# Who turns the attention squares: PE, or VectorE with a way through DRAM, in a two-layer graph kernel

## The chip, the cores and the metric

The kernel runs on one core of a Trainium2 chip. Its time is device microseconds of one execution. The engines are PE (TensorE; PEld is its weight loads), DVE (VectorE), ACT (ScalarE), POOL (GpSimd) and SP (SyncE, which here only issues DMAs).

## The reference

Layer 0 is a graph attention layer over 4096 nodes with 256 features and a dense 0/1 adjacency. Layer 1, where the change lies, does two steps of a top-p attention and of a graph walk:

```python
def _top_p_attention(X, W1, W2, W3):
    q = X @ W1.T @ W2.T
    k = X @ W3.T
    probs = softmax(q @ k.T / TAU, axis=-1)
    # keep, in every row, the largest probabilities up to a sum of TOP_P = 0.9
    ...
    A = probs * mask
    return A / maximum(A.sum(-1, keepdims=True), 1e-12)

R = S + eye(N);  R = R / R.sum(-1, keepdims=True)
Z = 0;  Xf = X;  Xa = X
for n in range(2):
    A = _top_p_attention(Xa, W1, W2, W3)
    Xf = R @ Xf
    Xa = A @ Xa
    Z = Z + Xf @ U1[n].T + Xa @ U2[n].T
h = X + Z
return (h - mean(h)) / sqrt(var(h) + LN_EPS) * ln_g + ln_b
```

Each layer is entered through a normalization and a relu, and added to its input.

## The kernel before

The 4096 rows are 32 blocks of 128 (NB = 32). The kernel's stages follow each other: layer 0, the first hop (`R @ X`, `graph_products`), step 0's attention over the 32 blocks, the second hop with the projections of step 1 put between its products, step 1's attention. Nearly all of it is under a manual schedule: every engine executes its instructions in the order in which the program writes them, and waits at the head of its queue for what it needs.

**One block of attention.** For block b, `exponentials` (ACT) makes the row block e of 128 x 4096 f32 from the logits (PE, `logits`). ACT counts against a first threshold (`first_probe`, four passes of 2048 columns), POOL works out the next threshold in some fifteen tiny instructions (`first_step`, its result is the tile c), DVE filters with it (`third_probe`, line L1015 in the profile, 128x4096), finds the cut (`candidates`: 18 MAX8 over the filtered row, then a chain of small operations, L1033 to L1052, with L1049 and L1050 in it), and zeroes what is under the cut (`masked`, L1058, 128x4096, in place in e). Then e is the left operand of `A @ X`, and PE needs it with the 4096 columns on the partitions: `turn` transposes four squares of 128x128 (L1124) into a PSUM tile and ACT copies them to SBUF (eT, L1126); `gather` multiplies them with four blocks of X and accumulates (L1132; each f32 product shows as two matmuls). There are eight such groups g of four squares.

**The order around it.** For each b the program writes `chosen_kept(b)` and then `attend(b)`:

```python
for b in range(NB - 1):
    chosen_kept(b)
    if b + AHEAD < NB:
        blocks[b + AHEAD] = began(n, b + AHEAD, G)
    attend(blocks[b], cur, blocks.get(b + AHEAD),
           beside.get(b, {}), [first] if b == 0 else ())
```

`attend(b)` has PE turn and gather block b, with the logits, exponentials and probes of block b + 3 (AHEAD) put between the groups; group g + 2 is turned before group g is gathered. `chosen_kept(b)` writes, in this order, candidates of b, `polished` of b - 3 (step 1: two POOL rows L1333 and L1334 and the output's DMA), third_probe of b + 1, `finish` of b - 2 (DVE: L1311 in step 0 with a store of z; L1314 and two statistics in step 1), `finish_scale` of b - 2 (POOL L1321 to L1325), `first_step` of b + 2 (POOL), `gathered` of b - 1 (step 1: three POOL rows L1150 to L1152), and masked of b (DVE). Blocks 0 to 2 of each step have their cut found earlier, in the hop before (`picks`). `began` loads the next query through SP (`swapped`), `loads` (SP) brings xf, and in step 1 v, z and x1.

**The states' products.** At the start of step 1, `projections` multiplies each block of the attention's states with both U2 matrices (`carried`, PE L797). Half of the result, v, is copied by ACT (L799) and stored by an ACT DMA; the other half replaces the states (DVE copy, L801). All this lies between the products of the second hop, whose own operands DVE and ACT prepare (L467, L468, five buffers).

Of the kernel before, what the change touches and what calls it, by code (L numbers as in the profile page):

```python
# [26 lines left out]
P = 128  # L27
# [29 lines left out]
def gat_then_top_p_diffusion(  # L57
# [100 lines left out]

    uv_d = dram.tile([H, P, NB, 2, W3 + 1], BF16, name="uv_d")
    s_d = dram.tile([H, N], F32, name="s_d")  # L160
    adj_d = dram.tile([NB // G0, P, NB, G0 * P], F32R, name="adj_d")
    with tc.tile_pool(name="l0", bufs=1) as l0, tc.tile_pool(name="l0s", bufs=2) as l0s, tc.tile_pool(name="l0o", bufs=1) as l0o:
        passing = ctx.enter_context(ExitStack())
# [613 lines left out]
    def projections(cur, n, G):  # L777
# [10 lines left out]
        lengths = small.tile([P, NB, 2], F32, name="lengths", bufs=1)  # L788
        u2 = S.u2.pop() if n > 0 else None

        def carried(xs, g, i):
            if n == 0:
                return
            b = 4 * g + i
            pt = ps3.tile([P, 4, P], F32, name="tp").rearrange("p a b -> p (a b)")
            for k in range(KC):
                nc.tensor.matmul(pt, xs[:, k, i, :], u2[:, k].rearrange("p n m -> p (n m)"), start=(k == 0), stop=(k == KC - 1))  # L797
            v = rows.tile([P, D], F32, name="part", bufs=3)
            nc.scalar.copy(v, pt[:, :D])  # L799
            nc.scalar.dma_start(block(v_d, b), v)  # L800
            nc.vector.tensor_copy(cur[:, b, :], pt[:, D:])  # L801

        for g in range(NB // 4):
            xs = l1e.tile([P, 3, 4, P], F32, name="xs", tag="e1")
# [250 lines left out]
    def masked(r):  # L1055

        kept, r.scale = col("kept"), col("scale")
        nc.vector.scalar_tensor_tensor(r.e, r.e, r.t, r.e, ALU.is_ge, ALU.mult, accum_out=kept)  # L1058
        nc.vector.reciprocal(r.scale, kept)
# [24 lines left out]
    def untied(r, z, work):  # L1084
# [18 lines left out]
        nc.vector.scalar_tensor_tensor(r.e, ties, r.t, r.e, ALU.mult, ALU.add, accum_out=kept)  # L1103
        nc.vector.reciprocal(r.scale, kept)

    def block(t, b):
        return t[ds(b, 1)].rearrange("o p d -> (o p) d")

    def loads(r):
        r.xf, r.part = rows.tile([P, KC, P], F32, name="xf"), rows.tile([P, D], F32, name="part", bufs=3)  # L1110
        nc.sync.dma_start(r.xf, xft_d[r.n][ds(r.b, 1)].rearrange("o p s i -> (o p) s i"))
        if r.n > 0:
            r.v = rows.tile([P, D], F32, name="xa")
            nc.sync.dma_start(r.v, block(v_d, r.b))
            nc.sync.dma_start(r.part, block(z_d, r.b))
            r.x1 = rows.tile([P, D], F32, name="x1", bufs=3)
            nc.sync.dma_start(r.x1, block(x1_d, r.b))
        r.acc = ps1.tile([P, 2, D], F32, name="acc")
        r.far = r.acc[:, 1, :]
# [9 lines left out]
    def gather(r, eT, g, cur):  # L1129
        for i in range(4):  # L1130
            j = 4 * g + i
            nc.tensor.matmul(r.acc[:, 0, :], eT[:, i, :], cur[:, j, :], start=(j == 0), stop=(j == NB - 1))  # L1132

    def scaled(r):
        if r.n + 1 < STEPS:
# [11 lines left out]

    def gathered(r):
        if r.n + 1 == STEPS:
            nc.gpsimd.tensor_tensor(r.part, r.part, r.v, ALU.add)  # L1150
            nc.gpsimd.tensor_tensor(r.x1, r.x1, ln_b_r, ALU.add)
            nc.gpsimd.tensor_tensor(r.part, r.part, r.xf.rearrange("p k i -> p (k i)"), ALU.add)  # L1152

    def attend(r, cur, ahead, between={}, eT=()):

        if ahead:
            ahead.pm = {}
        def start(c):
            if ahead:
                ahead.pm[c] = logits(ahead.q, ahead.kT, c)  # L1160
                exponentials(ahead, c)
        eT = list(eT) or [turn(r, 0)]
        start(0)
        loads(r)
        r.ri = rinv[:, r.b:r.b + 1]
        last = r.n + 1 == STEPS and r.b + 1 == NB
        if last:
            r.far = bank()[:, :D]
        eT.append(turn(r, 1))
        start(1)  # L1170
        for g in range(NB // 4):
            if g + 2 < NB // 4:
                eT.append(turn(r, g + 2))
            gather(r, eT[g], g, cur)
            if last and g == 4:
                contributed(r)
                weighed(r)
                gathered(r)
            if g < 2:
                start(2 + g)  # L1180
            elif g == 2 and ahead:
                summed(ahead)
            elif g in PROBED and ahead:
                first_probe(ahead, PROBED.index(g))
            if g in between:
                between[g]()
        if not last:
            contributed(r)
            weighed(r)
        scaled(r)  # L1190
# [193 lines left out]
    for n in range(STEPS):  # L1384
        cur = X
        G = SimpleNamespace()
        found = [table(f"found{i}") for i in range(3)]
        blocks = {}
        with tc.manual_schedule(engines=every):
            pieces = first_hop if n == 0 else hops(second)  # L1390
            filling, picking = fills(n, G, found, blocks), picks(n, found, blocks)
            done = 0 if n else NB - G0 - LOOK
            for i, _ in enumerate(pieces, 2 * done):
                if n > 0 and i % 6 == 1 and i // 6 < NB // 4:
                    g = i // 6
                    nc.sync.dma_start(cur[:, ts(g, 4), :], xa_d[ts(g, 4)].rearrange("b p d -> p b d"))
                if (n == 0 or i > 10) and i // 2 % NB != NB - 2:
                    next(filling, None)
                    if i // 2 % NB < NB - 3 or i % (2 * NB) == 2 * NB - 1:
                        next(picking, None)  # L1400
                if i == 2 * len(order) - 6:
                    first = turn(blocks[0], 0)
            weights(n)
            for _ in filling:
                next(picking, None)
            for _ in picking:
                pass

            def chosen_kept(b):

                r = blocks[b]
                if not hasattr(r, "kept"):
                    candidates(r, found)
                if b > 2:
                    polished(blocks.pop(b - 3))
                if b + 1 < NB and not hasattr(blocks[b + 1], "thirded"):
                    third_probe(blocks[b + 1])
                if b > 1:
                    finish(blocks[b - 2])
                    finish_scale(blocks[b - 2])  # L1420
                if b + 2 < NB and not hasattr(blocks[b + 2], "stepped"):
                    first_step(blocks[b + 2])
                if 0 < b < NB - 1:
                    gathered(blocks[b - 1])
                if not hasattr(r, "kept"):
                    masked(r)
                if 1 < b < NB - 1:
                    normal(blocks[b - 2])

            R = SimpleNamespace(n=n, kT=G.kT, qT=G.qT, nm=G.nm, table=found[0])  # L1430

            def last_chosen():
                chosen_kept(NB - 1)
                R.failed, R.undone = questioned(G, found)

            def looked():
                counted(R)
                chosen(R)

            def beginning():  # L1440
                normal(blocks[NB - 3])
                gathered(blocks[NB - 2])
                finish(blocks[NB - 2])
                finish_scale(blocks[NB - 2])

            def asked():
                R.count = number(R, R.undone)

            beside = {NB - 2: {5: last_chosen}, 0: dict(zip((0, 1, 3, 5, 6), S.turned))}
# [6 lines that stand above are left out]
            r = blocks[NB - 1]  # L1456

            def earlier():
                polished(blocks[NB - 3])
                finish_rows(blocks[NB - 2])  # L1460

            beside = {0: beginning, 1: looked, 3: earlier, 4: asked}
            if n + 1 < STEPS:
                second = hop_of(n + 1)
                beside.update({2: lambda: (both_weights(), begin(second, 5)), 5: lambda: split(second, 2), 6: lambda: (split(second, 5), own(second, 5))})
            attend(r, cur, None, beside)
            for m in range(second.begun if n + 1 < STEPS else 0):
                for s in range(KC):
                    graph_products(second, m, s, (0,))
            finish(r)  # L1470
            finish_scale(r)
            finish_rows(r)
        repaired(R, cur)
# [32 lines left out]
```

## Time and profile before

| | |
|---|---|
| median of 3 runs | 2820.71 us (2817.5 to 2821.74) |
| the profiled execution | 2820.09 us, span of its instructions 2818.1 us |
| granted TensorE clock, mean | 0.996 |
| L1132, gather | x4096, 948.0 us busy on PE |
| L1124, transposes | x2048, 306.4 us busy on PE |
| L1126, copies of the transposed squares | x512, 297.0 us busy on ACT |
| L1015 and L1058, third_probe and masked | x58 each, 261.4 and 259.0 us busy on DVE |
| step 0's attention, from block 0's end to block 31's | 1095.99 to 1766.81 us |
| step 1's attention, the same | 2136.86 to 2804.30 us |

The busy time of a group is the time in which at least one of its instructions ran; PE's matmuls overlap, so 948.0 us for 4096 is 0.23 us each though one lasts 0.38. Idle time is put down to what released the engine last. The time of an execution lies some 2 us above the span.

### The profile page before, as it was taken

The page shows a single profiled execution, that of the slowest core. Times are in us where ns is not written, and L with a number is a line of the kernel's source. Part 1 is how long each engine was busy: PE and PEld are TensorE (multiplying, and loading weights), DVE is VectorE, ACT ScalarE, POOL GpSimd, SP SyncE. Part 2 cuts the span into 40 slices and gives each one's busy share as a digit, 9 for nine tenths or more (in the row PEclk, how much of TensorE's full clock was granted, in tenths as well). Part 3 has the DMA queues.
Part 4 walks back from the last instruction along what each step waited for, and adds up shares of the span by engine and source line. Part 5 has one row for each costly group of instructions (what it writes and reads, how often), then busy time and mean ns, then how long its engine had stood idle before and what let it go on. Part 6 is the DMA issues. An engine that isn't in the chain of part 4 may idle for free. (4 is left out here: it accounts for less than half of the span.)

```text
span 2818.1 us, 51577 instructions
## 1 busy us (share of the span) xinstructions
PE 2772.0 (98%) x18791; PEld 2443.1 (87%) x18791; DVE 2164.6 (77%) x5067; ACT 1925.4 (68%) x3066; POOL 907.2 (32%) x1895
## 2 busy tenths in 40 slices
PE   6999999999999999999999999999999999999998
PEld 5899999999988888888888888667878888888887
DVE  8877878778654385999989997333574999999997
ACT  8867886879633636888888884232627878887882
POOL 7311121111011231223332231000304666666664
PEclk9999999999999999999999999999999999999999
DMA  9969597695376782000000002667991111111110
GB/s 204 255 247 197 210 233 196 228 203 217 143 229 213 242 305 94 21 21 21 27 20 21 21 24 69 217 196 239 332 348 50 32 34 40 31 32 32 37 34 26
DMA packets 174114, 376.44 MB, mean 134 GB/s; under 512 B 18198, under 2 KB 123542, under 8 KB 169750
## 3 DMA queue, kind: packets, MB, share of 16 engines
q1 hardware_dynamic: 142496, 271.12, 29.9%
q0 software_dynamic: 26112, 97.53, 13.8%
q10 hardware_dynamic: 5238, 4.35, 0.5%
q8 instruction: 153, 2.51, 0.4%
q14 instruction: 115, 0.94, 0.1%
HBM read 305.48 MB, written 113.57 MB: 149 GB/s over the span
## 5 line engine op out<-in xcount | busy, mean ns | idle before, releaser
L1132 PE MATMUL acc<-X,eT 128*128 128x256 f32 x4096 | 948.0, 379 | 0.0
L1132 PEld LDWEIGHTS acc<-X,eT 128*128 128x128 f32 x4096 | 748.1, 190 | 85.7
L400 PE MATMUL acc<-ut,m 128*128 128x195 bf16 (+1 forms) x8192 | 698.1, 246 | 1.2 <-DVE m L379 0.9
L400 PEld LDWEIGHTS <-m 128*128 128x128 fp8e4 x8192 | 696.8, 97 | 2.4 <-DVE m L379 1.5
L372 ACT ACTIVATE g<-sr,d_big 128x1024 uint8<-128x1024 f32 x448 | 473.0, 1135 | 9.9 <-DVE m L378 9.9
L947 ACT ACTIVATE e<-mm,nm 128x1024 f32<-128x1024 f32 x256 | 286.4, 1119 | 178.3 <-PE mm L763 167.4
L1126 ACT COPY eT<-tp 128x512 f32<-128x512 f32 x512 | 297.0, 581 | 80.1 <-PE tp L1124 79.8
L1033 DVE MAX8 cand<-big 128x8 f32<-128x228 f32 (+1 forms) x1152 | 348.3, 380 | 0.0
L646 PE MATMUL mm<-ar,hl 128*128 128x512 f32 x848 | 336.4, 407 | 3.8 <-DMA ar<-adj_d 1.7
L1015 DVE SCALAR_TENSOR_TENSOR big<-e,c 128x4096 f32<-128x4096 f32 x58 | 261.4, 4506 | 87.0 <-POOL c L1000 56.9
L646 PE MATMUL acc<-ar,hl 128*128 128x512 f32 x848 | 324.1, 393 | 1.3 <-DVE ar L490 1.3
L1124 PE MATMUL tp<-ident,e 128*128 128x128 f32 x2048 | 306.4, 273 | 5.3 <-ACT eT L1126 3.1
L1124 PEld LDWEIGHTS tp<-ident,e 128*128 128x128 f32 x2048 | 254.2, 141 | 65.7 <-ACT eT L1126 4.5
L378 DVE TENSOR_TENSOR m<-g,ax 128x512 uint32<-128x512 uint32 x256 | 188.7, 737 | 97.4 <-PE acc L400 76.9
L1058 DVE SCALAR_TENSOR_TENSOR e<-e,found 128x4096 f32<-128x4096 f32 x58 | 259.0, 4466 | 0.0
L954 ACT ACTIVATE void<-e,c 128x2048 int8<-128x2048 f32 x128 | 257.0, 2008 | 0.9
L954 ACT ACTIVATE void<-e,c1x 128x2048 int8<-128x2048 f32 x128 | 256.9, 2007 | 0.9
L971 POOL TENSOR_TENSOR sums<-sums 128x2 f32<-128x2 f32 x64 | 12.7, 199 | 623.7 <-ACT void L954 622.2
L379 DVE TENSOR_TENSOR m<-m,ax 128x512 uint32<-128x512 uint32 x256 | 183.2, 715 | 25.7 <-PE acc L400 0.5
L646 PEld LDWEIGHTS mm<-ar,hl 128*128 128x128 f32 x848 | 159.6, 188 | 43.7 <-issue 9.5
L763 PE MATMUL mm<-kT,qT 128*128 128x512 f32 x512 | 192.4, 457 | 1.5 <-ACT e L947 1.5
L646 PEld LDWEIGHTS acc<-ar,hl 128*128 128x128 f32 x848 | 159.3, 188 | 37.7 <-issue 4.1
(311 smaller groups left out, 3525.6 us busy)
## 6 DMA issues: line engine op xcount, KB each, us to landing
ar<-adj_d SPq DMA_DIRECT2D x212, 512.0 KB, 4.7
adj_d<-ax POOLq DMA_DIRECT2D x32, 2048.0 KB, 7.7
ut<-uv_d SPq DMA_DIRECT2D x60, 784.0 KB, 6.4
aru<-adj_d SPq DMA_DIRECT2D x44, 512.0 KB, 4.5
ax<-in_adj_t_dram POOLq DMA_DIRECT2D x32, 512.0 KB, 18.3
x<-xf_d SPq DMA_DIRECT2D x78, 128.0 KB, 5.2
xf<-xft_d SPq DMA_DIRECT2D x64, 128.0 KB, 2.3
sr<-s_d SPq DMA_DIRECT2D x15, 512.0 KB, 4.9
```

The costliest lines, as they stand in the source:

```text
L372: nc.scalar.activation(g[:, c, :], shared[k].sr, AF.Relu, scale=BIG, bias=d_big[:, h, j:j + 1])
L400: nc.tensor.matmul(shared[k].acc[i][:, t, :cols], m[t][:, c, ts(i, P)], shared[k].ut[j // QUARTER][:, j % QUARTER, t, :cols], start=(j == ...
L646: nc.tensor.matmul(A.acc[c][s], A.hl[m][:, t, ts(s, P)], A.ar[m][:, ts(c, 512)], start=(j == 0 and t == 0), stop=(j == NB - 1 and t == 1))
L763: nc.tensor.matmul(pm[:, h, :], q[t], kT[:, ds(h * (N // 2) + c * 512, 512)], start=(t == 0), stop=(t == 1))
L947: nc.scalar.activation(ev[:, :, c, :], r.pm[c], AF.Exp, bias=r.nm, accum_out=r.sums[:, c // 2, c % 2:c % 2 + 1])
L954: nc.scalar.activation(void, r.e[:, ts(h, N // 2)], (AF.Relu, AF.Sign)[i], bias=r.c1, scale=-1.0, accum_out=r.sums[:, h, 2 + i:3 + i])
L1015: nc.vector.scalar_tensor_tensor(big, r.e, r.c3, r.e, ALU.is_le, ALU.mult, accum_out=r.low3)
L1033: nc.vector.max(cand[:, s, :], big[:, edges[s]:edges[s + 1]])
L1058: nc.vector.scalar_tensor_tensor(r.e, r.e, r.t, r.e, ALU.is_ge, ALU.mult, accum_out=kept)
L1124: nc.tensor.transpose(pt[:, i, :], r.e[:, ts(4 * g + i, P)], ident)
L1126: nc.scalar.copy(eT, pt)
L1132: nc.tensor.matmul(r.acc[:, 0, :], eT[:, i, :], cur[:, j, :], start=(j == 0), stop=(j == NB - 1))
```

## The change

Blocks 3 to 30 of each step no longer have all their squares turned by PE. `sent(b)`, written after `masked(b)`, has DVE transpose the last 8 (step 0) or 4 (step 1) squares in pieces of 32x32, written so that a piece's neighbours lie 8 or 4 elements apart. Four DMAs store the result to DRAM and one loads it back with the pieces on the right partitions, all on SP's queue; `gather` takes these squares from there, with a step of 8 or 4 elements, and `turn` is not called for them. Both tiles take turns in the four buffers that the hops use for the adjacency.

In the states' products DVE adds z to v as it takes it from PSUM, with z loaded and the sum stored through POOL's queue, and ACT copies the other half. So step 1 loads one tile less and `gathered` has one POOL row less. `polished(b - 3)` moves behind `finish_scale(b - 2)`.

```diff
+    turned_ds = [dram.tile([NB, 4, 32, 4, k * 32], F32, name=f"turned{k}_d") for k in (8, 4)]
...
+        zs = {}
+
+        def fetched(b):
+            if n > 0 and b < NB:
+                zs[b] = rows.tile([P, D], F32, name="z", tag="xf")
+                nc.gpsimd.dma_start(zs[b], block(z_d, b))
+
+        for b in range(2):
+            fetched(b)
...
-            nc.scalar.copy(v, pt[:, :D])
-            nc.scalar.dma_start(block(v_d, b), v)
-            nc.vector.tensor_copy(cur[:, b, :], pt[:, D:])
+            nc.vector.tensor_tensor(v, pt[:, :D], zs.pop(b), ALU.add)
+            nc.gpsimd.dma_start(block(v_d, b), v)
+            fetched(b + 2)
+            nc.scalar.copy(cur[:, b, :], pt[:, D:])
...
+    SENT = (8, 4)
+
+    def sent(r):
+        many = SENT[r.n]
+        wide, turned_d = many * 32, turned_ds[r.n]
+        stage = rp.tile([P, G0 * P], F32, name="staged", tag="ar", bufs=4)
+        nc.vector.transpose(stage[:, :4 * wide].rearrange("p (c s b) -> p c b s", c=4, b=many),
+                            r.e[:, ds((NB - many) * P, many * P)].rearrange("p (b c r) -> p c b r", b=many, c=4))
+        landed = rp.tile([P, G0 * P], F32, name="landed", tag="ar", bufs=4)
+        for c in range(4):
+            nc.sync.dma_start(turned_d[r.b, c].rearrange("r q x -> q r x"), stage[:, ts(c, wide)])
+        nc.sync.dma_start(landed[:, :4 * wide], turned_d[r.b].rearrange("c r q x -> (c r) (q x)"))
+        r.landed = landed[:, :4 * wide].rearrange("p (i b) -> p b i", b=many)
...
-            r.v = rows.tile([P, D], F32, name="xa")
-            nc.sync.dma_start(r.v, block(v_d, r.b))
-            nc.sync.dma_start(r.part, block(z_d, r.b))
+            nc.sync.dma_start(r.part, block(v_d, r.b))
...
-            nc.tensor.matmul(r.acc[:, 0, :], eT[:, i, :], cur[:, j, :], start=(j == 0), stop=(j == NB - 1))
+            nc.tensor.matmul(r.acc[:, 0, :], r.landed[:, j - NB + SENT[r.n]] if eT is None else eT[:, i, :], cur[:, j, :], start=(j == 0), stop=(j == NB - 1))
...
-            nc.gpsimd.tensor_tensor(r.part, r.part, r.v, ALU.add)
...
-                eT.append(turn(r, g + 2))
+                eT.append(None if hasattr(r, "landed") and 4 * (g + 2) >= NB - SENT[r.n] else turn(r, g + 2))
...
-                if b > 2:
-                    polished(blocks.pop(b - 3))
                 if b + 1 < NB and not hasattr(blocks[b + 1], "thirded"):
                     third_probe(blocks[b + 1])
                 if b > 1:
                     finish(blocks[b - 2])
                     finish_scale(blocks[b - 2])
+                if b > 2:
+                    polished(blocks.pop(b - 3))
...
                 if not hasattr(r, "kept"):
                     masked(r)
+                    if b < NB - 1:
+                        sent(r)
```

## The prediction

> **What bounds the kernel now.** I read the engine totals first, then the waits of each engine in the two attention stretches, then the instructions in order of time. In the page's first rows the reader is to see that PE is busy for 98% and that the lines touched (transposes L1124, gather L1132) are its costliest with L400; so time taken off PE could shorten the run, if nothing else ends later.
>
> ```profile
> PE 2772.0 (98%) x18791; PEld 2443.1 (87%) x18791; DVE 2164.6 (77%) x5067; ACT 1925.4 (68%) x3066; POOL 907.2 (32%) x1895
> L1132 PE MATMUL acc<-X,eT 128*128 128x256 f32 x4096 | 948.0, 379 | 0.0
> L1124 PE MATMUL tp<-ident,e 128*128 128x128 f32 x2048 | 306.4, 273 | 5.3 <-ACT eT L1126 3.1 <-DVE e L1058 1.1 <-DVE ns_i_u L920 1.0
> ```
>
> Then step 0's attention in order of time (start, length, engine, line, idle before). DVE repeats its block every 21.91 us (1302.46 to 1324.37), of which it idles 1.51 for POOL's c; PE never stops.
>
> ```profile
> 1302.46 4.49 DVE L1015 SCALAR_TENSOR_TENSOR big<-e,c 128x4096 f32<-128x4096 f32 x1 [1.52 <-POOL c L1000]
> 1307.12 0.58 PEld L1124 LDWEIGHTS tp<-ident,e 128*128 128x128 f32 x4
> 1307.67 1.60 PEld L1132 LDWEIGHTS acc<-X,eT 128*128 128x128 f32 x8
> 1309.29 0.57 PEld L1124 LDWEIGHTS tp<-ident,e 128*128 128x128 f32 x4
> 1309.83 5.05 PEld L1132 LDWEIGHTS acc<-X,eT 128*128 128x128 f32 x24
> 1324.37 4.49 DVE L1015 SCALAR_TENSOR_TENSOR big<-e,c 128x4096 f32<-128x4096 f32 x1 [1.51 <-POOL c L1000]
> ```
>
> In step 1 the period is the same 21.9 us, but DVE has no idle time. Two small operations stand out: L1049 and L1050 take 0.59 and 0.79 us, against 0.19 and 0.27 in step 0, and end just as POOL's L1333 and L1334 end: DVE is held there by POOL's rows, 0.92 us a block. L1321, one column, takes 4.36 us on POOL because it starts under DVE's L1058: the hold goes both ways.
>
> ```profile
> 2504.28 4.36 POOL L1321 TENSOR_SCALAR rs<-mv 128x1 f32<-128x1 f32 x1 [6.12 <-DVE mv L150]
> 2508.48 0.08 DVE L1058 DVE_READ_ACCUMULATOR e<-e,found 128x1 f32 x1
> 2518.51 0.74 POOL L1333 TENSOR_TENSOR part<-part,ln_g_r 128x256 f32<-128x256 f32 x1
> 2518.70 0.59 DVE L1049 TENSOR_SCALAR drop<-cum 128x48 f32<-128x48 f32 x1
> 2519.33 0.73 POOL L1334 TENSOR_TENSOR part<-part,x 128x256 f32<-128x256 f32 x1
> 2519.33 0.79 DVE L1050 CUSTOM_DVE_ANT_0 work<-drop,best 128x48 f32<-128x48 f32 x1
> 2771.64 1.06 PE L1124 MATMUL tp<-ident,e 128*128 128x128 f32 x8 [1.12 <-DVE e L1058]
> ```
>
> The last of these is the one block start at which PE waits for DVE: block 30 of step 1. So DVE's own work is 21.91 - 1.51 = 20.40 us a block in step 0 and 21.90 - 0.92 = 20.98 in step 1. DVE stands right behind PE.
>
> **PE: what is removed.** A transposed group with its gather takes 1309.29 - 1307.12 = 2.17 us, a gather alone 5.08/3 = 1.69 (L1132's run of 24 from 1309.83 to 1314.91), so a group of four transposes is 0.48 us. Blocks 3 to 30 lose two groups in step 0 and one in step 1 (28 blocks each): PE could repeat every 21.91 - 0.96 = 20.95 and 21.43 us. ACT loses as many copies of 0.58 us; its queue has waits for PE in every block, so this is worth nothing by itself.
>
> **DVE: what is added.** One 32x32 transpose of 1024 elements a partition in step 0, 512 in step 1, behind L1058 and in front of the next block's MAX8 chain. No row shows a transpose. Low end: L370, 1024 f32 in 751 ns. Nearest: L1058, the same tile, 4096 elements at 1.04 ns; with the 0.16 us that L828 (512 elements, 693 ns) has beyond its elements, 1.07 + 0.16 = 1.23 us and 0.53 + 0.16 = 0.69. High end: the output is written 32 bytes apart (16 in step 1). Rows with steps that wide are tiny (the view of single lines; times are min/median/max ns):
>
> ```profile
> L1037 DVE TENSOR_REDUCE found<-cand x64: 174/184/191, 996.0 to 2777.1; 128x1 f32<-128x18 f32 x64
> L847 DVE TENSOR_REDUCE km<-lengths x2: 178/178/178, 903.3 to 1924.4; 128x1 f32<-128x32 f32 x2
> L425 DVE RECIPROCAL rden<-st x16: 193/196/198, 137.6 to 784.4; 128x8 f32<-128x8 f32 x16
> L431 DVE RECIPROCAL rinv<-rinv x4: 202/203/203, 138.6 to 681.1; 128x8 f32<-128x8 f32 x4
> ```
>
> L1037 reads 18 elements 32 bytes apart in 184 ns; L847, 32 elements 8 bytes apart, would be 178 - 14 x 1.04 = 163 at 18, so the wide step costs up to 21/18 = 1.1 ns an element, 2.19 in all: 2.40 and 1.28 us. But L425, eight elements far apart, is no slower than L431 with eight adjacent. I take 1.23 and 0.69 and keep 0.75 (0.48 for half the elements) and 2.40 (1.28) as ends.
>
> [...]
>
> PE reads the landed squares with the same step as weights. A load by itself takes at most 0.126 us (L808, eight in 1.02), its slot in the gather is 0.211; doubled it would stick out 0.04 us x 16 = 0.65 in step 0 and x 8 = 0.33 in step 1, giving PE 21.60 and 21.76: still about DVE's time. I take nothing.
>
> **The sum, step 0.** DVE's period becomes 20.40 + 1.23 = 21.63, more than PE's 20.95: DVE becomes the bound. From block 3's L1058 to block 30's lie 27 periods. The first gains nothing: DVE would come to L1015 at 1149.06 - 1.51 + 1.23, and still waits for a c that nothing earlier has moved. 26 x (21.91 - 21.63) = 7.3. PE began block 30 about 0.65 us after its squares were ready and will now start at once; that block's own gather is 0.96 shorter. Step 0: 8.9 us. PE's unused cover is 0.7 us a block.
>
> **Step 1.** L1058 of block 3 began at 2173.32, of block 30 at 2767.03: 593.7 us. After: 27 x (20.98 + 0.69 = 21.67) = 585.1, and 0.48 in block 30: 9.1 us. This needs POOL out of DVE's way. In the new order POOL's rows behind L1321 are two of L1322/L1325, polished's two (1.5), first_step (6.7, as from 2509.80 to 2516.49) and gathered's two (1.4), the addition of v being gone: counted from L1058's end, POOL finishes 10.8 us later, and L1049 comes at 2518.70 - 2508.48 + 0.69 = 10.9. The 0.92 goes, with hardly any margin. c is there at 9.4, L1015 needs it at 11.8.
>
> **Moved and hidden.** SP now carries five more DMAs a block in front of the query loads and xf, the fifth waiting for the four stores. Stores go out 3 us into the block; at 0.5 each, the 4.7 us that 512 KB loads take, and as much for the stores, the squares land at 12 to 14 us. Group 6 comes at 17, group 7 of step 1 at 19: hidden; without that cover the lateness falls on PE. Behind them, xf (2.3 us to land) is needed at 19, the query in the next block. In hop 2, DVE's addition and ACT's copy swap: both 0.42. z comes by POOL's queue, 4.4 to 4.6 us to land for 128 KB, plus two issues of 0.55 and 0.42 of the addition: 6.0, against 6.6 between the call that asks and the one that uses it. A late z holds DVE up to a microsecond or two, in front of which L468's splits lie four hop steps ahead: nothing, with 0 to 8 us as bounds. Step 1's loads lose one DMA.
>
> Sum: 8.9 + 9.1 = 18 us. The profiled execution took 2820.1 (span 2818.1), 0.6 under the median of the runs: 2802.
>
> **Rivals.**
> *The wide step costs VectorE a cycle an element.* L1037 speaks for it, L425 and L431 against. Periods 22.80 and 22.26: step 0 27 x 0.89 - 1.6 = +22.4, step 1 601.0 - 593.7 - 0.5 = +6.8: 2849. It decides from 1.48 ns an element, 1.68 us for the transpose of step 0, where gain and loss cancel.
> *POOL's rows slide under L1015 in step 1.* Early in the step L1151 lasts 4.90 us for that reason, L1015 4.93, and the next DVE row waits 1.30 for L1152: 1.75 a block. It decides if gathered ends 1 us later than I count. Step 1 is then 27 x 23.42 - 593.7 - 0.5 = +38, step 0 stays: 2849.
> *The transpose is as quick as L370.* Periods 21.15 and 21.46 (PE 21.43): 26 x 0.76 + 1.6 + 14.3 + 0.5 = 36: 2784.
> *A balance* near 1.6 us of transpose, or half of the POOL hold staying: within 0.2%, which is about what a measurement of this kernel can tell from no change (5.6 us).
>
> **How the numbers follow.** Forecast 0.47, quick transpose 0.11, wide step 0.25, POOL under L1015 0.08, balance 0.06, late squares or a late z (above 2826) 0.03. Faster 0.58, same 0.06, slower 0.36. The forecast's own range is 2794 to 2812 (0.1 us of DVE a block is 5.3 us). With both signs holding weight, the range runs from the quick transpose to the wide step: 2784 to 2850.
>
> **What would show it.** The transpose's mean against 1.23 and 0.69 us; L1015's period 21.6 in both steps, with no wait for c in step 0; PE waiting 0.2 to 0.7 us a block for L1058's squares; L1049 and L1050 near 0.2 and 0.3 in step 1; 428 copies at L1126's place in ACT's groups instead of 512 (56 and 28 fewer); no PE wait for landed. A transpose above 1.7 us, or L1015 near 4.9 in step 1, makes it wrong.

## The result and the profile after

The changed kernel takes 2832.39 us (median of 6 executions, 2830.1 to 2833.22) against 2820.56 (6 executions, 2817.5 to 2821.74): a ratio of 1.0042, 95% interval 1.0030 to 1.0053. It is slower by 11.8 us where 18 us of gain were forecast; the time lies inside the range, the sign is wrong. The profiled execution took 2833.22 us (span 2831.4), 13.1 more than the one of before.

The totals of the page of after, and its rows for gather and the transposes on PE (busy us, mean ns, idle before and what ended most of it):

```profile
PE 2761.8 (98%) x18455; PEld 2441.8 (86%) x18455; DVE 2220.1 (78%) x5123; ACT 1894.2 (67%) x2982; POOL 945.0 (33%) x1927
L1156 PE MATMUL acc<-X,eT 128*128 128x256 f32 x3424 | 791.1, 380 | 0.0
L1148 PE MATMUL tp<-ident,e 128*128 128x128 f32 x1712 | 258.2, 274 | 28.8 <-DVE e L1070 23.8
```

The removal happened: 1712 transposes instead of 2048. (The 672 matmuls that read the landed squares are a group of their own, so L1156's row is smaller by more than it lost.) What is new is the last column: PE now waits 23.8 us for DVE's L1070, where it waited 1.1. The timeline shows when. Step 0 of after (start, length, engine, line, idle before):

```profile
1396.09 4.48 DVE L1027 SCALAR_TENSOR_TENSOR big<-e,c 128x4096 f32<-128x4096 f32 x1
1399.70 3.90 PEld L1156 LDWEIGHTS acc<-X,landed 128*128 128x128 f32 x16
1405.52 0.63 PE L1148 MATMUL tp<-ident,e 128*128 128x128 f32 x4 [0.76 <-DVE e L1070]
1405.59 2.18 DVE L1124 STREAM_TRANSPOSE staged<-e 128x1024 f32<-128x1024 f32 x1
1407.60 5.38 DVE L1045 MAX8 cand<-big 128x8 f32<-128x227 f32 x18
1418.45 4.48 DVE L1027 SCALAR_TENSOR_TENSOR big<-e,c 128x4096 f32<-128x4096 f32 x1
```

DVE repeats its block every 22.36 us (1396.09 to 1418.45) and no longer waits for c. PE runs out of work and waits 0.76 us for the squares, up to 1405.52; from block 3 to block 30 of step 0 it waits 16.2 us for them. The transpose lasts 2.18 us and moves the next row on the queue by 2.01 (1405.59 to 1407.60), where 1.23 was forecast. The same in step 1 of after, and the start of block 30 there:

```profile
2563.76 0.63 PE L1148 MATMUL tp<-ident,e 128*128 128x128 f32 x4 [0.15 <-DVE e L1070]
2563.83 1.13 DVE L1124 STREAM_TRANSPOSE staged<-e 128x512 f32<-128x512 f32 x1
2564.77 5.41 DVE L1045 MAX8 cand<-big 128x8 f32<-128x227 f32 x18
2574.76 0.19 DVE L1061 TENSOR_SCALAR drop<-cum 128x48 f32<-128x48 f32 x1
2783.38 1.06 PE L1148 MATMUL tp<-ident,e 128*128 128x128 f32 x8 [2.65 <-DVE e L1070]
```

The transpose of 512 elements moves the queue by 0.94 us, not 0.69; L1061 (before: L1049) takes 0.19 us instead of 0.59, so POOL's hold on it is gone. The block takes 21.96 us. The views of single lines of after (min/median/max ns, first and last start) show that both engines that meet the wide step pay, DVE in writing and PE in reading:

```profile
L1124 DVE STREAM_TRANSPOSE staged<-e x56: 1099/1592/2221, 1137.9 to 2783.4; 128x1024 f32<-128x1024 f32 x28, 128x512 f32<-128x512 f32 x28
...
L1156 PEld LDWEIGHTS acc<-X,eT x3424: 190/190/338, 1077.6 to 2823.8; 128*128 128x128 f32 x191
L1156 PEld LDWEIGHTS acc<-X,landed x672: 307/334/338, 1158.5 to 2802.9; 128*128 128x128 f32 x168
```

A weight load of a landed square, whose columns lie 32 or 16 bytes apart, takes 334 ns (median); one of a square that PE turned takes 190.

Where the time went, cut at the starts of L1058 (before) and L1070 (the others), in us. The last column is the decisive experiment, told below:

| stretch | before | forecast | after | the change with a step of two elements |
|---|---|---|---|---|
| to block 3 of step 0 | 1131.96 | | 1133.26 | 1131.32 |
| block 3 to 30, step 0 | 591.67 | 584.3 | 602.88 | 581.87 |
| to block 3 of step 1 | 449.69 | | 449.02 | 448.50 |
| block 3 to 30, step 1 | 593.71 | 585.1 | 593.61 | 586.08 |
| to the end of the span | 51.07 | | 52.63 | 52.13 |

Step 0 lost 11.2 us, step 1 gained nothing. The other stretches together differ by 2.2.

### The profile page after: what moved, and what is told of

Same layout as the page of the kernel before. It is cut to its first block, busy times and chain, and to the rows that moved or that the text cites. A ratio compares the mean times of both kernels' runs of the same rounds, so it can differ in the third digit from the quotient of the medians.

```text
span 2831.4 us, 51275 instructions
## 1 busy us (share of the span) xinstructions
PE 2761.8 (98%) x18455; PEld 2441.8 (86%) x18455; DVE 2220.1 (78%) x5123; ACT 1894.2 (67%) x2982; POOL 945.0 (33%) x1927
## 5 line engine op out<-in xcount | busy, mean ns | idle before, releaser
L1156 PE MATMUL acc<-X,eT 128*128 128x256 f32 x3424 | 791.1, 380 | 0.0
L1156 PEld LDWEIGHTS acc<-X,eT 128*128 128x128 f32 x3424 | 628.7, 191 | 73.3
L1150 ACT COPY eT<-tp 128x512 f32<-128x512 f32 x428 | 248.4, 582 | 96.3 <-PE tp L1148 96.2
L1148 PEld LDWEIGHTS tp<-ident,e 128*128 128x128 f32 x1712 | 209.7, 141 | 91.4 <-PE acc L1166 32.5
L1148 PE MATMUL tp<-ident,e 128*128 128x128 f32 x1712 | 258.2, 274 | 28.8 <-DVE e L1070 23.8
L1070 DVE SCALAR_TENSOR_TENSOR e<-e,found 128x4096 f32<-128x4096 f32 x58 | 259.0, 4465 | 0.0
L966 ACT ACTIVATE void<-e,c1x 128x2048 int8<-128x2048 f32 x128 | 256.4, 2003 | 2.6
L966 ACT ACTIVATE void<-e,c 128x2048 int8<-128x2048 f32 x128 | 256.6, 2005 | 1.8
L983 POOL TENSOR_TENSOR sums<-sums 128x2 f32<-128x2 f32 x64 | 39.4, 616 | 583.4 <-ACT void L966 583.4
L1344 POOL TENSOR_SCALAR rs<-mv 128x1 f32<-128x1 f32 x32 | 127.4, 3983 | 208.0 <-DVE mv L150 208.0
```

The costliest lines, as they stand in the source:

```text
L966: nc.scalar.activation(void, r.e[:, ts(h, N // 2)], (AF.Relu, AF.Sign)[i], bias=r.c1, scale=-1.0, accum_out=r.sums[:, h, 2 + i:3 + i])
L1148: nc.tensor.transpose(pt[:, i, :], r.e[:, ts(4 * g + i, P)], ident)
L1150: nc.scalar.copy(eT, pt)
L1156: nc.tensor.matmul(r.acc[:, 0, :], r.landed[:, j - NB + SENT[r.n]] if eT is None else eT[:, i, :], cur[:, j, :], start=(j == 0), stop=(j = ...
```

## The experiments

The theory after the result: DVE and PE pay for an access whose neighbours lie far apart, and the transpose thereby takes some 2 ns an element instead of 1; all else in the sum holds. Its rivals: the 32x32 transpose of f32 takes 2 ns an element however its data lie; the time is lost in the rest of the change (z, POOL's order, the DMAs); DVE is slow because the traffic of the squares disturbs it.

**The costs by themselves.** In front of the kernel before, DVE transposes, adds, and PE loads weights, at steps of 1, 2, 4 and 8 elements:

```diff
+    for _ in range(3):
+        for k in (8, 4, 2):        # the changed kernel's pattern, step k
+            nc.vector.transpose(tout[:, :128 * k].rearrange("p (c s b) -> p c b s", c=4, b=k),
+                                tin[:, :128 * k].rearrange("p (b c r) -> p c b r", b=k, c=4))
+        for k in (8, 4):           # pieces adjacent
...
+        for k in (1, 2, 4, 8):     # additions, output or input with step k
...
+    for k in (1, 2, 4, 8):         # weights with step k
+        for j in range(8):
+            nc.tensor.matmul(pb[:, :256], tin[:, :128 * k].rearrange("p (i s) -> p i s", s=k)[:, :, 0], tin[:, :256], start=(j == 0), stop=(j == 7))
```

> The kernel before with rows put in front of it that measure the disputed costs alone: VectorE transposes of f32 with the output's neighbours 8, 4 and 2 elements apart, adjacent (two sizes), in natural order, and of bf16; additions of 512 f32 with the output, then one input, 1, 2, 4 and 8 elements apart; matmuls with weights 1, 2, 4 and 8 elements apart. Theory A: f32 transposes of 1024 near 1.1 us when adjacent or in natural order and 2.1 at a step of 4 or 8; additions 0.69 us adjacent, 1.2 at steps of 4 and 8; weight loads 0.19 at steps 1 and 2, 0.33 at 4 and 8. Theory B: 2.1 us for every f32 transpose of 1024, 1.1 for bf16; additions 0.69 throughout. The time is that of before plus about 60 us of these rows and says nothing.

DVE's timeline of this run (L113 has the step, L116 not, L118 is 1024 elements in their natural order):

```profile
6.13 1.98 DVE L113 STREAM_TRANSPOSE tout<-tin 128x1024 f32<-128x1024 f32 x1
9.08 1.06 DVE L113 STREAM_TRANSPOSE tout<-tin 128x512 f32<-128x512 f32 x1
11.12 0.40 DVE L113 STREAM_TRANSPOSE tout<-tin 128x256 f32<-128x256 f32 x1
12.56 1.21 DVE L116 STREAM_TRANSPOSE tout<-tin 128x1024 f32<-128x1024 f32 x1
```

From 256 elements at a step of 2 to 512 at a step of 4 the time grows by 0.66 us where 0.27 would do at 1.04 ns an element; 1024 elements at a step of 8 take 1.98, with adjacent output 1.21. In this run the price therefore sets in between a step of 8 bytes (free) and one of 16 bytes, and does not grow on DVE from 16 to 32: over three rounds it is 0.35 to 0.37 us for the 512 elements at 16 bytes (adjacent 0.71) and 0.77 us for the 1024 at 32 (adjacent 1.21 to 1.25), some 0.7 to 0.75 ns an element on top of 1.04. That is less than the doubling that theory A had. It is no matter of the transpose: additions of 512 f32 took 0.69 us at steps of 1 and 2 and 1.06 to 1.12 at 4 and 8, whether the input or the output had the step. Nor of DVE alone, as PE's loads at steps of 2, 4 and 8 show (single lines in three windows of this run):

```profile
L127 PEld LDWEIGHTS pb<-tin x10: 195/197/197, 11.0 to 12.9; 128*128 128x128 f32 x10
...
L127 PEld LDWEIGHTS pb<-tin x11: 329/329/329, 14.5 to 16.8; 128*128 128x128 f32 x11
...
L127 PEld LDWEIGHTS pb<-tin x11: 337/337/338, 18.5 to 20.9; 128*128 128x128 f32 x11
```

At a step of one a load took 190 ns. With no traffic of squares at all, the transposes with the wide step take 1.98 to 2.02 and 1.06 to 1.08 us here, against 2.03 to 2.22 and 1.10 to 1.15 in the changed kernel. The rival "always 2 ns" falls, and "traffic" is left with the difference, some 0.15 and 0.04 us, for which no run shows a cause. The kernel took 2869.83 us in one execution, the probes included; that time says nothing.

**The pieces adjacent.** The same change, with the step moved from DVE and PE into the DMAs, which now store runs of 128 bytes instead of 1 KB:

```diff
-        nc.vector.transpose(stage[:, :4 * wide].rearrange("p (c s b) -> p c b s", c=4, b=many),
+        nc.vector.transpose(stage[:, :4 * wide].rearrange("p (c b s) -> p c b s", c=4, b=many),
...
-            nc.sync.dma_start(turned_d[r.b, c].rearrange("r q x -> q r x"), stage[:, ts(c, wide)])
+            nc.sync.dma_start(turned_d[r.b, c].rearrange("r b q s -> q r b s"), stage[:, ts(c, wide)].rearrange("p (b s) -> p b s", b=many))
...
-        r.landed = landed[:, :4 * wide].rearrange("p (i b) -> p b i", b=many)
+        r.landed = landed[:, :4 * wide].rearrange("p (b i) -> p b i", b=many)
```

> Edit of the changed kernel: VectorE writes its 32x32 pieces with neighbours adjacent (no wide step), the four stores put them in place in runs of 128 bytes, the load is contiguous, and PE reads its weights without a step. Theory A (the wide step costs a second cycle, on VectorE and on PE's weight loads): transposes near 1.1 and 0.55 us instead of 2.18 and 1.12, weight loads of the landed squares 190 ns instead of 334, DVE periods about 21.4 in both steps: some 17 to 20 us under before, 2801 to 2804, if the squares land in time. Theory B (a transpose of f32 takes two cycles an element in any layout): transposes stay at 2.18 and 1.12, only the weight loads fall to 190; DVE still sets the period at 22.35 and 21.96, and the time stays at 2831 to 2834. Either way the 4096 short runs could land late; then PE waits for landed and the time goes up.

Measured: 2908.91 us, ratio 1.0318 (1.0302 to 1.0333). Both times that were expected missed, since what had been put in as a caveat came true: in step 0 the squares come late. The transposes take 1.25 and 0.71 us at most, 0.15 more than theory A had and far from theory B's 2.18 and 1.12, and the loads of landed squares take 190 ns. But in step 0 of this run's timeline:

```profile
1393.47 8.79 SPq L1128 DMA_DIRECT2D turned_d<-staged  x4
1407.37 0.32 SPq L1129 DMA_DIRECT2D landed<-turned_d  x1
1411.15 3.32 PEld L1156 LDWEIGHTS acc<-X,landed 128*128 128x128 f32 x16 [2.78 <-DMA landed<-turned_d]
```

The load is issued at 1407.37, 13.9 us after the first store (1393.47), and PE waits for it; over the run PE waits 84 us for landed squares and its weight loads 95. In the changed kernel the load is issued 8.1 us after the first store (1407.80 to 1415.89), and PE and its weight loads together wait 1.2 us for landed squares in all. The changed kernel's timeline has the same four stores:

```profile
1407.80 2.34 SPq L1128 DMA_DIRECT2D turned_d<-staged  x4
```

So the time goes into the issuing of the stores on SP's queue, 8.79 us instead of 2.34. From the end of the last store's issue to the load's issue it is 5.1 us here and 5.8 there: that part does not grow with short runs. In step 1, where half as much is stored, PE waits for no landed square, the block takes 21.6 to 21.7 us against 21.96, and the 27 periods from block 3 to 30 take 586.0 us, where 585.1 had been forecast. So this run confirms the durations, and for step 1 the sum; in step 0 it shows the price of a hidden transfer whose cover is gone.

**Pairs.** The layout between the two: two squares alternate, so DVE and PE step by two elements (8 bytes), and the DMAs store runs of 256 bytes. All else as in the changed kernel:

```diff
-        nc.vector.transpose(stage[:, :4 * wide].rearrange("p (c s b) -> p c b s", c=4, b=many),
-                            r.e[:, ds((NB - many) * P, many * P)].rearrange("p (b c r) -> p c b r", b=many, c=4))
+        nc.vector.transpose(stage[:, :4 * wide].rearrange("p (c g s t) -> p c g t s", c=4, g=many // 2, t=2),
+                            r.e[:, ds((NB - many) * P, many * P)].rearrange("p (g t c r) -> p c g t r", g=many // 2, t=2, c=4))
...
-        r.landed = landed[:, :4 * wide].rearrange("p (i b) -> p b i", b=many)
+        r.landed = landed[:, :4 * wide].rearrange("p (g i t) -> p g t i", t=2, i=P)
```

> The changed kernel (eight squares in step 0, four in step 1) with the step of 2. Theory A: transposes 1.23 and 0.71 us, DVE 21.5 us a block in step 0 and 21.55 in step 1, as the forecast had it: about 2802, if 2048 runs of 256 bytes land in time. From the landings seen (8 us of stores for 512 runs, about 15 for 4096) they would come 1 to 2 us late for group 6: then 21.5 to 22.5 in step 0 and 2803 to 2825, with PE waiting for landed.

Measured: 2802.67 us (2800.56 to 2803.85), ratio 0.9942 (0.9927 to 0.9957). A step of 2 elements in place of 8 and 4 turns the loss of 11.8 us into a gain of 16.5, and the time is the one that had been forecast for the change. Its timeline in step 0:

```profile
1389.69 3.44 PEld L1156 LDWEIGHTS acc<-X,landed 128*128 128x128 f32 x16
1394.72 0.63 PE L1148 MATMUL tp<-ident,e 128*128 128x128 f32 x4 [0.33 <-DVE e L1070]
1394.78 1.25 DVE L1124 STREAM_TRANSPOSE staged<-e 128x1024 f32<-128x1024 f32 x1
1395.95 5.40 DVE L1045 MAX8 cand<-big 128x8 f32<-128x227 f32 x18
1396.06 6.53 SPq L1128 DMA_DIRECT2D turned_d<-staged  x4
```

The transpose moves the queue by 1.17 us, DVE's block takes 21.54 us (forecast 21.63) in step 0 and 21.66 (21.67) in step 1; the sixteen landed loads take 3.44 us instead of 3.90. DVE stays the bound, as forecast. The load of the squares is issued 10.3 us after the first store (1396.06 to 1406.33) instead of 8.1, 6.5 of them the issuing of the stores, yet PE and its weight loads together wait for landed squares only 4.1 us in the whole run.

**Nothing sent.** The call of `sent` is taken out; z in the states' products and POOL's order stay as in the changed kernel, and PE turns all squares:

```diff
                     masked(r)
-                    if b < NB - 1:
-                        sent(r)
```

> Edit of the changed kernel: no square is sent, PE turns them all; z in the states' products and the moved POOL rows stay. If all of the loss comes from the squares, PE sets both steps again at 21.91 us a block, DVE's rows L1061 and L1062 (the small ones that POOL held, 0.59 and 0.79 us before) are 0.19 and 0.27, and the time is that of before within 4 us, 2816 to 2822. If z or POOL's order costs something by itself, it is above 2824.

Measured: 2818.22 us, ratio 0.9994 (0.9985 to 1.0003): the rest of the change neither costs nor brings anything that can be measured, and the rival that puts the loss there falls. DVE's and POOL's timelines of this run in step 1 show something else:

```profile
2516.13 0.73 POOL L1174 TENSOR_TENSOR x<-x,ln_b_r 128x256 f32<-128x256 f32 x1
2516.27 0.63 DVE L1063 TENSOR_SCALAR work<-drop 128x48 f32<-128x48 f32 x1
2516.82 0.73 POOL L1175 TENSOR_TENSOR part<-part,xf 128x256 f32<-128x256 f32 x1
2516.94 0.67 DVE L1064 CUSTOM_DVE_ANT_0 work<-best,work 128x48 f32<-128x48 f32 x1
```

POOL's hold on DVE is not gone here, it has moved: L1061 and L1062 take 0.19 and 0.27 us, but L1063 and L1064, 0.19 and 0.21 in step 0, take 0.63 and 0.67 under POOL's `gathered` rows and end with them. That is 0.9 us again, and DVE's block is 21.90 us as before. POOL's rows end 12 us after L1070 here, against 10.6 in the changed kernel; its L983 waits 1.3 us for ACT's L966, a wait that it does not have there.

**POOL's order.** `polished` is put back behind `candidates`, everything else as changed:

```diff
                     candidates(r, found)
+                if b > 2:
+                    polished(blocks.pop(b - 3))
...
                     finish_scale(blocks[b - 2])
-                if b > 2:
-                    polished(blocks.pop(b - 3))
```

> The changed kernel with polished back in its old place, in front of third_probe. If POOL's rows then hold L1061 and L1062 on DVE again (0.9 us a block, as before the change) while DVE sets the period of step 1, that step gets 27 x 0.5 to 0.9 longer: 2845 to 2857. If the move was worth nothing: 2830 to 2834.

Measured: 2832.38 us, ratio 1.0048 (1.0032 to 1.0063), the changed kernel's time: of the two outcomes written down, the one in which the move was worth nothing. The hold does not come back. In this run POOL's last row ends at 2507.27, 10.6 us after L1070's end, and L1061 starts at 2507.83; in the changed kernel `gathered`'s last row ends at 2508.37 and L1061 starts at 2508.87. Both orders hold the same rows, so POOL is done as early in one as in the other. With the transpose on DVE's queue the move is worth nothing; without it, it was not tried.

**Four squares in both steps**, still at a step of four elements:

```diff
-    SENT = (8, 4)
+    SENT = (4, 4)
```

> Edit of the changed kernel: four squares instead of eight in step 0 too. The transpose then takes about 0.94 us of DVE's queue in step 0, DVE 20.40 + 0.94 = 21.34 a block, under PE's 21.43 plus what the stepped weight loads add (16 slots of 0.03 less: about 0.25): PE would set some 21.7 us, step 0 gains 27 x 0.2 + 0.5 and the time is 2814 to 2818. If something other than DVE's transpose slowed step 0 (SP's stores, the landing), the time stays above 2824.

Measured: 2810.15 us, ratio 0.9966 (0.9954 to 0.9979), some 4 us better than the near end of what was expected. A block of step 0 from this run's timeline:

```profile
1407.94 4.48 DVE L1027 SCALAR_TENSOR_TENSOR big<-e,c 128x4096 f32<-128x4096 f32 x1 [0.22 <-POOL c L1012]
```

With a transpose of 1.12 us instead of 2.18 PE bounds step 0 again, at 21.60 us a block: from block 3 to 30 PE shows 0.2 us of idle time in all and DVE waits 4.6 us for c (in 19 of the blocks, 0.2 us or so each). So DVE stands close behind. Step 1 goes at about 21.96 as in the changed kernel. The same layout thus wins or loses by how much of it DVE has room for.

**Both, four squares and pairs**, the pairs' edit and this:

```diff
-    SENT = (8, 4)
+    SENT = (4, 4)
```

> Four squares in both steps, and a step of 2 elements instead of 4: VectorE writes two squares in alternation, the stores move runs of 256 bytes, PE reads its weights 8 bytes apart. Theory A (a step of 16 bytes or more costs a second cycle, one of 8 bytes none): transposes 0.71 us instead of 1.12, landed weight loads near 196 ns instead of 329; step 0 bound by PE at 21.43 to 21.5 us (21.60 with four squares at a step of 4), step 1 by DVE at 21.5 to 21.6 (21.95): 2800 to 2805. If the step of 2 also costs: as with four squares at a step of 4, 2810. Late landing: PE waits for landed and the time rises above 2812.

Measured: 2799.2 us (2798.35 to 2800.85), ratio 0.9932 (0.9918 to 0.9945), the lowest median of all and 0.8 us under the range expected; its lead of 3.5 us over the pairs alone is not clear of the noise, as the two intervals overlap. Its timeline in step 0 has DVE waiting, 10.6 us over the 27 blocks, and PE not (0.2):

```profile
1385.06 4.48 DVE L1027 SCALAR_TENSOR_TENSOR big<-e,c 128x4096 f32<-128x4096 f32 x1 [0.40 <-POOL c L1012]
```

PE's block is 21.47 us against 21.60 in the run with four squares at a step of four: eight landed loads of 197 ns instead of 329. Step 1 goes at 21.66 against 21.96. 27 x 0.13 + 27 x 0.30 = 11.6 us, and the two runs differ by 11.0.

## Why the prediction was wrong

**The step that failed** is the price of the transpose: "I take 1.23 and 0.69 and keep 0.75 (0.48 for half the elements) and 2.40 (1.28) as ends." On DVE's queue it cost 2.01 and 0.94. The 0.78 and 0.25 us a block that were missing put the two stretches of 27 periods 18.6 and 8.5 us over their forecast, 27 of the 30 us between forecast and result. The row that pointed to it was in the prediction: L1037, 18 elements 32 bytes apart, with up to 1.1 ns an element beyond an adjacent read (the costs by themselves: 0.7 to 0.75). I let L425 and L431 outvote it, eight elements each. At 1 ns an element, eight would cost 8 ns more, and 193 to 198 against 202 to 203 ns on two different tiles can't tell that from other differences of the two. L1037's 21 ns, against L847 on another tile, are the better evidence for having more elements, though not free of the same doubt.

In the runs f32 that lie 8 bytes apart cost DVE nothing (0.69 us for 512 additions, as with adjacent data); at 16 or 32 bytes apart the additions took 1.06 to 1.12 us, in reads and in writes, and one of PE's weight loads took 329 to 338 ns against 190. That is 1.5 to 1.8 times, not the 1.95 times of the prediction's high end for the transpose (2.40 us against 1.23). For adjacent data 512 elements more took 1.245 - 0.711 = 0.53 us more to transpose (the costs by themselves), 1.04 ns each, which is also what the prediction read from L1058 for an element.

**The rival that named it** put 2849, since it took 2.40 and 1.28 us, with 1.15 ns an element for the step. The transposes lasted 2.15 and 1.12 us on average and moved the queue by less than that, as their ends overlap the next row (2.18 us long, 2.01 on the queue). With 2.01 and 0.94 its periods are 20.40 + 2.01 = 22.41 and 20.98 + 0.94 = 21.92, measured 22.36 and 21.96. Its turning point of 1.68 us for step 0's transpose holds by what was run: 2.01 loses, 1.17 wins.

**The rest of the sum held.** The pairs run has the transpose at 1.17 and 0.63 us on the queue, close to the forecast's price, and gives 581.87 and 586.08 us for the 27 periods of the steps against 584.3 and 585.1. So DVE's own work of 20.40 and 20.98, and DVE becoming the bound, were right. PE's block was 21.03 us while it had a lead, against 20.95. That the pairs run meets the forecast time within 1 us is luck in part: step 0's periods are 2.4 us better than forecast, step 1's 1.0 worse, and the stretches outside them gain 0.8 us instead of the 2.1 that were counted.

**PE's weight loads with a step** were taken at nothing, with a bound of 0.65 us a block. They cost (3.90 - 3.44) = 0.46 us a block in step 0: while PE still had a lead its blocks took 21.40 us, and 21.03 with pairs. (The bound doubled 0.126 us, the distance between L808's loads; a load of gather itself lasts 190 ns, and 334 with the step.) In the changed kernel this lies under DVE's 22.36; where PE bounds, as with four squares, it costs.

**The hold of POOL** went in the changed kernel, as forecast, but the new order has no part in it. Its rows end 10.6 to 10.7 us after L1070 (forecast 10.8) and L1061 comes 0.5 us later, where a margin of 0.1 had been forecast; in the pairs run, whose transpose is as short as forecast, the margin is 0.15 to 0.27. The run that moves the rows back keeps the hold away as well. With v's row gone but no transpose the hold came back on the next two rows, so the missing row by itself is not enough; in the runs without the hold DVE comes later, by the transpose. Whether v's row would have to go as well was not tried.

**z and the landing** were right. From block 31's L1166 in step 0 to block 0's in step 1 (before: L1142) it took 370.4 us, before 370.05. The squares were asked for 10.4 us after the block's start, and PE and its weight loads together waited for them 1.2 us in all.

**The end of step 1** is a small miss. PE waits 2.65 us at block 30's start (before 1.12), as DVE is the bound up to it, and then takes 20.0 us from its first transposes to L1166 (before: 18.6 to L1142), though it has one group less. The granted clock is 0.50 there from 2785.7 to 2789.0, 0.99 from 2783.3 up to it and 1.00 behind it, to 2803.3; the eight matmuls of gather in that time last 3.26 us instead of 1.89. Half of the clock for 3.3 us is 1.65 us, most of what is missing.

## What to carry to other kernels

A price per element has to be read from the row with the most elements in the same layout, and a row with eight elements can't contradict it: ask how large the difference would be in that row if the suspected cost were real. Where a layout puts f32 neighbours 16 bytes or more apart for one engine, try the layout that keeps two of them together (here a transpose of 1024 elements moved DVE's queue by 1.17 us instead of 2.01, and a weight load took 197 ns instead of 329 to 338) before moving the whole step into the DMAs, whose short runs took the queue longer to issue here (8.79 us instead of 2.34). Before work is moved to an engine that stands right behind the bound, write down its room per block in microseconds (here 1.5 and 0.9) and take only what fits.

## What the runs showed of the hardware that was not expected

- The price of a step set in at the same step on both engines: f32 at 8 bytes apart cost nothing on DVE (0.69 us for 512 additions) and 3 to 4% on PE (190 to 197 ns a load); at 16 bytes 1.06 to 1.12 us and 329 ns; at 32 bytes no more than that on DVE, 338 ns on PE. No run had a step of 12 bytes. 1024 bf16 took 1.21 us to transpose, 1024 f32 with adjacent output 1.21 to 1.25.
- Stores in short runs held the queue that issued them: four stores of 128 KB took SP 2.34 us to issue in runs of 1 KB, 6.53 in runs of 256 bytes and 8.79 in runs of 128 bytes. From then to the load's issue it took 5.8, 3.7 and 5.1 us.
- POOL's two-input rows of 128x256 held some DVE operations to their own end and not others: without squares sent, L1063 went from 0.19 to 0.63 us under L1174, while MAX8 and MATCH_REPLACE8 kept their 0.31 and 0.29 us under the same row in the changed kernel.
- After PE's wait of 2.65 us in block 30 of step 1, its granted clock was 0.91 over the next 20 us: half for some 3.3 us, then full. With pairs, after a wait of 2.48 us there, it was 0.91 over 20 us as well. The eight matmuls of gather that come next after the wait took 3.26 us in the changed kernel, 2.80 with pairs, 3.62 with four squares and pairs (wait 2.47) and 3.17 with POOL's rows back (wait 2.65), where eight of them take 1.89 elsewhere. The kernel before, with a wait of 1.12 us, kept 1.00 over the next 18.6. That the wait is the cause was not tested by itself.
